# Window attention with channels split 128 and 64, sums copied by sixths for the output projection, and transposes set a piece ahead of the weighted sums

## The chip, the cores and the metric

The kernel runs on one core of a Trainium2 chip. The metric is the time of one execution on the device, in microseconds (us), a median of runs. Everything is fp32.

## The reference, cut to what matters

The network takes an image batch of 8 samples, 56 x 56 pixels, 192 channels, and runs four residual layers. Layers 0 and 1 are Toeplitz mixers, layer 2 is a ConvNeXt block, and layer 3 is a window attention. Each gets its input normalized by groups of six channels (`_gn`). The change concerns layer 3 alone:

```python
x = jnp.roll(x, (-3, -3), (1, 2))                  # x is the group-normalized input
q, k, v = (a.reshape(b, 6, nw, 49, 32) for a in (x @ Wq, x @ Wk, x @ Wv))
scores = jnp.einsum('bhnqd,bhnkd->bhnqk', q, k) * 32 ** 0.5 + bias   # with two masks
attn = jax.nn.softmax(scores, axis=-1)
out = jnp.einsum('bhnqk,bhnkd->bhnqd', attn, v).reshape(b, n_h, n_w, -1)
out = jnp.roll(out @ Wfc + bfc, (3, 3), (1, 2))    # then added to the layer's input
```

The reshape of `q`, `k` and `v` is a plain one: it reads a sample's 3136 tokens of 192 numbers as one row of numbers and cuts it anew into 6 heads of 64 windows of 49 vectors of 32. So one token holds six vectors of 32 ("sixths"), and a window takes 49 vectors that follow one another in that row. The output `out` is read back in the same way, so the output projection again contracts six vectors of 32 for every token.

## The kernel before, in words

Layers 0 to 2 (`tno_layers`, `convnext`) are as they were and come first. `attention` then runs 16 units: the 8 samples, and for each two halves `hh`. A unit is four strips `i` of seven image rows (392 tokens each), one strip from every quarter of the image, so that the four strips fill four groups of 32 partitions. The 192 channels lie as two blocks of 96 (`CH = 96`, `chunked`).

`project(b, hh)` is a generator, so its pieces can be laid between others. It loads the strips to `raw` (`L916`), normalizes and rolls them to `xr` (`L57` on VectorE for the first block of channels, `L928` on ScalarE for the second), and yields. Then it makes the values: for each strip four matmuls over each block of channels (`L938`, 98 tokens stationary, 192 columns), a copy to `vs` on ScalarE (`L946`), a store to DRAM (`vd`, `L948`) and loads of `v` that cut the tokens anew into windows (`L959`). Then, after a yield each, queries and keys (`L973`): for each sixth, half of the strip and block of channels four matmuls, one for each strip, 32 output columns each, side by side in the four column groups. The results go to `f`, laid out token by token with the six sixths inside (`L985` on VectorE, `L983` on ScalarE).

Attention proper runs by thirds `g` of 16 windows in each strip. `scores` multiplies queries and keys (`L997`), adds the bias (`L1009`), and does the softmax: maximum (`L1018`, VectorE), difference (`L1019`, GpSimd), exponential (`L1020`, ScalarE), sum and reciprocal (`L1022`, `L1023`, VectorE), product (`L1024`, GpSimd). `weighted` transposes the result (`L1034`), copies it to `et` (`L1044` on VectorE for one half, `L1042` on ScalarE for the other), multiplies it with the values (`L1052`) and copies the sums to `ot` (`L1059`, VectorE), where, as in `f`, the sixth is the inner index. `out` projects to the 192 channels (`L1071`): for each block of 96 channels and each sixth, four matmuls of 32 rows, one for each strip, side by side in the row groups; the moving operand is

```python
oj = ot.rearrange("p (t j) -> p t j", j=6)
...
oj[qd, :, j],
```

every sixth number of a partition. Then VectorE adds bias and residual in place into `raw` (`L1083`), and `raw` goes to the output (`L1090`).

The order of the pieces is written out by hand in the loop over units. In each third come the scores of the unit; in the first third the previous unit's `out`; then one step of the next unit's `project`; then `weighted` of the third before. What is left of `project` runs before the last `weighted`. Every engine works in program order; a PSUM tile (`bank2`) is two banks, and there are four of them, used in turn. All loads and stores of the attention are issued from one queue (SP), also in order, and a load or store that must wait for something holds up those behind it.

Of the kernel before, what the change touches and what calls it, by code (L numbers as in the profile page):

```python
# [12 lines left out]
F32 = mybir.dt.float32  # L13
AF = mybir.ActivationFunctionType
ALU = mybir.AluOpType
# [7 lines left out]
CH = 96  # L23
# [14 lines left out]
def chunked(ap):  # L38

    return ap.rearrange("(k p) t -> p k t", p=CH)  # L40


class Net:
# [11 lines left out]

    def gn_apply(self, out, x, gn, b, k):
        self.nc.vector.tensor_scalar(  # L57
            out, x, gn[:, k, b, 0:1], gn[:, k, b, 1:2], ALU.mult, ALU.add
        )
# [800 lines left out]
    def attention(self, L, xs, gnd, ys, vd):  # L860
# [6 lines left out]
        ST = HT // 4  # L867
# [3 lines left out]
        with tc.tile_pool(name="at", bufs=2) as p, tc.tile_pool(  # L871
# [4 lines left out]
            gn = one("gn", [CH, 2, B, 2])  # L876
            for b in range(B):
                nc.sync.dma_start(gn[:, :, b, :], chunked(gnd[b * C : (b + 1) * C, :]))
            ws = []
            for n in ("Wq", "Wk", "Wv"):  # L880
                w = one(n, [CH, 2, C])
                nc.sync.dma_start(w, chunked(inp[f"{L}_{n}"]))
                ws.append(w)
# [5 lines left out]
            bfc = one("bfc", [CH, 2])  # L889
# [16 lines left out]

            def project(b, hh):

                raw = p.tile([CH, 2, 4, 7, W], F32, name="raw", bufs=3)
                for i in range(4):
                    r = 14 * i + 7 * hh + 3
                    for a, n in ((0, 7),) if r + 7 <= H else ((0, H - r), (H - r, 7 - H + r)):
                        at = (r + a) % H * W
                        nc.sync.dma_start(  # L916
                            raw[:, :, i, a : a + n, :].rearrange("p k h w -> p k (h w)"),
                            chunked(xs[b])[:, :, at : at + n * W],
                        )
                xr = p.tile([CH, 2, 4 * 7, W], F32, name="xr", bufs=1)  # L920
                rw = raw.rearrange("p k i h w -> p k (i h) w")
                for k in range(2):
                    for c, n, c2 in ((3, 53, 0), (0, 3, 53)):
                        to, of = xr[:, k, :, c2 : c2 + n], rw[:, k, :, c : c + n]
                        if k == 0:
                            self.gn_apply(to, of, gn, b, k)
                        else:
                            nc.scalar.activation(  # L928
                                to, of, AF.Identity, bias=gn[:, k, b, 1:2], scale=gn[:, k, b, 0:1]
                            )  # L930
                xf = xr.rearrange("p k h w -> p k (h w)")
                yield
                v = p.tile([128, 4, 24, 32], F32, name="v", bufs=2)
                for i in range(4):
                    pv = bank2()
                    for s in range(4):
                        for k in range(2):
                            nc.tensor.matmul(  # L938
                                pv[:ST, s // 2, s % 2 * C : (s % 2 + 1) * C],
                                xf[:, k, i * HT + s * ST : i * HT + (s + 1) * ST],  # L940
                                ws[2][:, k, :],
                                start=k == 0,
                                stop=k == 1,
                            )
                    vs = p.tile([ST, 2, 2 * C], F32, name="vs", bufs=3)
                    nc.scalar.copy(vs, pv[:ST, :, : 2 * C])  # L946
                    t0 = i * (T // 4) + hh * HT
                    nc.sync.dma_start(  # L948
                        vd[b][t0 : t0 + HT, :].rearrange("(s p) d -> p s d", p=ST),
                        vs.rearrange("p a (c d) -> p (a c) d", d=C),  # L950
                    )
                    for par in range(2):
                        for q0, n in ((0, 48), (48, 1)):
                            of = bass.AP(
                                vd[b].tensor,
                                vd[b].offset + t0 * C + (WR * par + q0) * 32,
                                [[32, n], [2 * WR * 32, 24], [1, 32]],
                            )
                            nc.sync.dma_start(v[64 * par + q0 : 64 * par + q0 + n, i], of)  # L959
                fs = []  # L960
                for m in range(2):
                    yield
                    f = p.tile([128, HR + 16], F32, name=f"f{m}", bufs=2)
                    if m == 0:
                        nc.gpsimd.memset(f[:, HR:], 0.0)
                    for th in range(2):
                        for j0, nj in ((0, 4), (4, 2)):
                            pq = bank2()
                            for j in range(nj):
                                for k in range(2):  # L970
                                    for i in range(4):
                                        t0 = i * HT + th * (HT // 2)
                                        nc.tensor.matmul(  # L973
                                            pq[32 * i : 32 * i + 32, j // 2, j % 2 * 196 : (j % 2 + 1) * 196],
                                            ws[m][:, k, 32 * (j0 + j) : 32 * (j0 + j) + 32],
                                            xf[:, k, t0 : t0 + HT // 2],
                                            start=k == 0,
                                            stop=k == 1,
                                        )
                            to = view(f, th * (HR // 2) + j0, [[6, 196], [2, nj // 2], [1, 2]])  # L980
                            of = view(pq, 0, [[1, 196], [512, nj // 2], [196, 2]])
                            if j0:
                                nc.scalar.copy(to, of)  # L983
                            else:
                                nc.vector.tensor_copy(to, of)  # L985
                    fs.append(f)
                return raw, v, fs[0], fs[1]

            def scores(hh, g, i, qf, kf):

# [29 lines left out]
                nc.scalar.activation(e3, e3, AF.Exp)  # L1020
                sm = p.tile([128, 16], F32, name="sm", bufs=6)
# [3 lines left out]
                return e  # L1025

            def weighted(g, es, v, ot):

                po = bank2()
                for i in range(2):  # L1030
                    pt = bank2()
                    for c in range(2):
                        for m in range(4):
                            nc.tensor.transpose(  # L1034
                                pt[:113, c, m * 128 : m * 128 + 113],
                                es[i].rearrange("p c n k -> p c (n k)")[:113, c, m * 128 : m * 128 + 113],
                                self.ident[:113, :113],
                            )
                    et = p.tile([113, 8, 113], F32, name="et", bufs=3)
                    ev = pt.rearrange("p c (m q) -> p (c m) q", q=128)[:113, :, :113]  # L1040
                    if i:
                        nc.scalar.copy(et, ev)  # L1042
                    else:
                        nc.vector.tensor_copy(et, ev)  # L1044
# [17 lines left out]
                )  # L1062

            def out(b, hh, raw, ot):
                oj = ot.rearrange("p (t j) -> p t j", j=6)
                for k in range(2):
                    fs = [bank2(), bank2()]
                    for j in range(6):
                        for i in range(4):
                            qd = slice(32 * i, 32 * i + 32)  # L1070
                            nc.tensor.matmul(  # L1071
                                fs[i // 2][:CH, i % 2, :HT],
                                wfc[qd, j, k * CH : (k + 1) * CH],
                                oj[qd, :, j],
                                start=j == 0,
                                stop=j == 5,
                            )
                    for i in range(4):

                        for c, n, c2 in ((0, 53, 3), (53, 3, 0)):  # L1080
                            to = raw[:, k, i, :, c2 : c2 + n]
                            of = fs[i // 2][:CH, i % 2, :HT].rearrange("p (h w) -> p h w", w=W)
                            nc.vector.scalar_tensor_tensor(  # L1083
                                to, of[:, :, c : c + n], bfc[:, k : k + 1], to, ALU.add, ALU.add
                            )
                for i in range(4):
                    r = 14 * i + 7 * hh + 3
                    for a, n in ((0, 7),) if r + 7 <= H else ((0, H - r), (H - r, 7 - H + r)):
                        at = (r + a) % H * W
                        nc.sync.dma_start(  # L1090
# [186 lines left out]
```

## Time and profile before

| what | value |
|---|---|
| time, median of 3 | 6828.79 us (6823.43 to 6830.44) |
| span of the profiled execution | 6818.4 us |
| TensorE busy with matmuls, whole span | 6075.2 us (89%) |
| first scores of the attention start at | 5691.2 us |
| mean granted TensorE clock, whole span | 0.932 |

The busiest groups of the attention, 5600 us to the end, are `L1071` (269.1 us), `L938` (174.9 us), `L973` for the queries (157.2 us) and for the keys (138.8 us). A busy time of TensorE counts a stretch once, however many matmuls run side by side in it, and a matmul's record in the profile is longer than the time after which the next may start; so rates are better taken from how many records pass in a stretch of the chain of waits. One fp32 matmul leaves two records there. In a group's line, "32*96" is rows by columns of the array, "32x392" the operand that streams through.

### The profile page before, as it was taken

What the parts mean: (1) busy time and instruction counts of PE and PEld (TensorE: products, weight loads), DVE (VectorE), ACT (ScalarE), POOL (GpSimd) and SP (SyncE); (2) the same over time, 40 slices, a digit from 0 to 9 for tenths busy, and PEclk for the clock granted to TensorE, in tenths of its full rate; (3) what the DMA queues carried; (4) which work ended last, traced back from release to release, by engine and by line L of the source; (5) the groups of instructions that cost most, each with busy time, mean ns of one, the idle gap of its engine ahead of it and who ended that gap; (6) DMA issues with size and microseconds to landing.
All of it is one profiled execution on the core that took longest, in us unless ns stands there. A gap on an engine that the chain in (4) does not pass through costs nothing.

```text
span 6818.4 us, 150579 instructions
## 1 busy us (share of the span) xinstructions
PE 6075.2 (89%) x68076; PEld 4712.2 (69%) x68076; DVE 2921.2 (43%) x4778; ACT 2033.1 (30%) x2730; POOL 616.1 (9%) x806
## 2 busy tenths in 40 slices
PE   5999878988998898898888899989988997999998
PEld 4777766777777787776777778854475446666665
DVE  6555544443554443555344344250125014444454
ACT  2344432223443222443232222223322332222221
POOL 0000000000000000000000000000000002222222
PEclk9999998988999888999888999999989998999998
DMA  7459886676675676765877654631172114232231
GB/s 240 118 163 249 238 211 186 188 192 176 184 199 166 179 210 193 178 202 161 218 212 213 176 177 139 225 101 41 45 250 95 41 45 94 59 81 66 59 87 38
DMA packets 1223457, 1038.86 MB, mean 152 GB/s; under 512 B 453265, under 2 KB 1180609, under 8 KB 1208737
## 3 DMA queue, kind: packets, MB, share of 16 engines
q1 hardware_dynamic: 810248, 599.79, 31.1%
q10 hardware_dynamic: 378648, 247.74, 13.9%
q0 software_dynamic: 33920, 181.71, 8.5%
q8 instruction: 535, 8.77, 0.5%
q14 instruction: 106, 0.86, 0.0%
HBM read 692.26 MB, written 336.85 MB: 151 GB/s over the span
## 4 chain that ended last, share of the span: by engine, by line
PE 73%; DVE 9%; DMA 6%; ACT 5%; issue 4%; ACTq 2%; SPq 1%; POOL 0%; DVEq 0%; POOLq 0%
PE bank L233 14%; PE pp L789 6%; PE bank L446 5%; PE bank L347 5%; PE bank L456 5%; PE bank L330 5%; PE bank L973 4%; PE pc L708 4%; PE bank L1071 4%; PE po L812 4%; PE bank L461 2%; PE bank L938 2%; PE po L817 2%; PE bank L478 2%; DVE t L242 2%
## 5 line engine op out<-in xcount | busy, mean ns | idle before, releaser
L233 PE MATMUL bank<-wq,t 64*128 64x256 f32 (+5 forms) x8000 | 1318.7, 372 | 63.5 <-ACT ot L337 48.8
L233 PEld LDWEIGHTS bank<-wq,t 64*128 64x128 f32 (+3 forms) x8000 | 1039.7, 189 | 316.6 <-issue 101.8
L242 DVE TENSOR_TENSOR t<-bank,wq 128x1024 f32<-128x1024 f32 (+2 forms) x500 | 540.3, 1113 | 502.6 <-PE bank L233 501.4
L347 PE MATMUL bank<-ident,ot 120*128 120x120 f32 x4032 | 562.2, 303 | 204.1 <-DVE s L350 52.9
L278 ACT ACTIVATE t<-t 128x2048 f32<-128x2048 f32 (+1 forms) x300 | 438.4, 1480 | 972.2 <-DVE t L242 809.5
L347 PEld LDWEIGHTS bank<-ident,ot 120*128 120x128 f32 x4032 | 501.4, 161 | 270.8 <-DVE s L350 65.4
L330 PE MATMUL bank<-q,tm 56*64 56x112 f32 x18432 | 518.5, 265 | 73.8 <-issue 35.3
L330 PEld LDWEIGHTS bank<-q,tm 56*64 56x64 f32 x18432 | 480.0, 138 | 108.7 <-issue 56.0
L490 ACT ACTIVATE t<-bank,wo 128x448 f32<-128x448 f32 x448 | 247.7, 635 | 1020.3 <-PE bank L461 728.2
L497 DVE TENSOR_TENSOR t<-t,t 128x896 f32<-128x896 f32 x224 | 241.1, 1088 | 678.5 <-ACT t L490 676.6
L337 ACT COPY ot<-bank 128x896 f32<-128x896 f32 x576 | 481.7, 917 | 100.6 <-PE bank L330 99.7
L446 PE MATMUL bank<-t,wo 128*128 128x224 f32 x1792 | 414.6, 388 | 77.6 <-ACT t L490 45.8
L789 PE MATMUL pp<-z,w 64*128 64x448 f32 (+1 forms) x1344 | 454.8, 562 | 0.0
L446 PEld LDWEIGHTS bank<-t,wo 128*128 128x128 f32 x1792 | 363.5, 210 | 111.4 <-ACT t L490 46.8
L254 DVE TENSOR_TENSOR t<-t 128x1024 f32<-128x1024 f32 (+1 forms) x300 | 280.7, 954 | 302.5 <-ACT t L278 263.0
L456 PE MATMUL bank<-t,wo 128*128 128x224 f32 x1792 | 367.8, 358 | 6.2 <-DVE t L497 6.0
L456 PEld LDWEIGHTS bank<-t,wo 128*128 128x128 f32 x1792 | 343.8, 193 | 11.0 <-DVE t L497 5.7
L789 PEld LDWEIGHTS pp<-z,w 64*128 64x128 f32 (+1 forms) x1344 | 197.2, 190 | 218.3 <-issue 182.4
L826 DVE TENSOR_TENSOR o<-o,x 128x1344 f32<-128x1344 f32 x28 | 43.6, 1558 | 683.3 <-ACT o L823 683.3
L350 DVE COPY s<-bank 128x784 f32<-128x784 f32 x288 | 264.3, 967 | 132.6 <-PE bank L347 93.0
L353 DVE TENSOR_TENSOR s<-s,bank 128x784 f32<-128x784 f32 x288 | 263.7, 966 | 117.1 <-PE bank L347 117.0
L708 PE MATMUL pc<-xt,cm 112*112 112x108 f32 (+2 forms) x3072 | 307.1, 262 | 0.9 <-issue 0.9
(136 smaller groups left out, 7226.6 us busy)
## 6 DMA issues: line engine op xcount, KB each, us to landing
q<-qv ACTq DMA_DIRECT2D x36, 3584.0 KB
L_sum<-s POOLq DMA_DIRECT2D x288, 392.0 KB, 7.2
t<-L_sum SPq DMA_DIRECT2D x112, 1008.0 KB
qv<-t SPq DMA_DIRECT2D x192, 512.0 KB
cm<-in_L_cm SPq DMA_DIRECT2D x96, 896.0 KB
tm<-L_tab ACTq DMA_DIRECT2D x144, 392.0 KB
q<-qv SPq DMA_DIRECT2D x36, 1568.0 KB
q<-qv ACTq DMA_DIRECT2D x36, 1568.0 KB
```

What stands on the lines that cost most here:

```text
L233: nc.tensor.matmul(pp[:m, b, 256 * j : 256 * j + k], x[rows, j, 2 if part else b, s : s + m], w[rows, part, c0 + c : c0 + c + k],  start=p ...
L242: nc.vector.tensor_add(z[:m, c : c + k, :], view(pp[:m], 0, [[1, k], [256, 4]]), view(bias[:m], c0 + c, [[1, k], [0, 4]]),)
L254: nc.vector.tensor_mul(prod[:m, :k], half[:, :, 0], half[:, :, 1])
L278: nc.scalar.activation(z[:m, :k, :], z[:m, :k, :], AF.Silu)
L330: nc.tensor.matmul(pt[64 * s : 64 * s + 64, r, j * 112 : (j + 1) * 112], tm[rows, c * H : c * H + 64], q[rows, PR * s : PR * s + PR, 4 * c ...
L337: nc.scalar.copy(view(ot, 4 * g, [[112 * 32, 2], [32, 112], [1, 4]]), view(pt, 0, [[512, 2], [1, 112], [112, 4]]),)
L347: nc.tensor.transpose(pz[:, i, :120], ot[:120, at : at + 128], self.ident[:120, :120])
L446: mm(gs[c // 2][:, b, c % 2 * 256 : c % 2 * 256 + N], pw[:, 0, 128 * c : 128 * c + 128], xn[:, b], start=c % 2 == 0, stop=False,)
L456: mm(P[:, b, :N], ow[:, c, 0:128], g[:, 4 * b + c], start=c == 0, stop=False)
L708: nc.tensor.matmul(pc[:, i, 4 * m0 : 4 * m1], cm[:112, i % 4, k, :], xt[:, m0 - 1 + k : m1 - 1 + k, g + i, :], start=n == 0 and i % 4 == 0 ...
L789: nc.tensor.matmul(phs[c, s], w0[rows, part, 128 * c : 128 * c + 128], z[rows, Z[2 if part else s], :], start=part == flip, stop=part != flip,
L812: nc.tensor.matmul(po[s], w1[:, c, 0:128], h[:, s, c, :], start=c == 0, stop=c == 5)
```

## The change

The channels are split 128 and 64 in place of 96 and 96, as the layer before leaves its group norm (`gn3`). The first 128 stand in `xa`, and the last 64 twice in `xb`: partitions 0 to 63 hold rows 0 to 3 of each strip, partitions 64 to 127 rows 3 to 6. A matmul over 128 channels uses the whole height of the array; those over 64 channels use one half of its rows each, so that the two halves of a strip can go side by side. In the output projection, 128 channels are made at once for the whole strip, and the last 64 in two column groups, one for each half of a strip.

`weighted` now also copies the sums from `ot` to `oj` on ScalarE, one sixth after the other, so that the output projection streams numbers that lie side by side. `scores` is cut in two (`divide` holds the second part of the softmax), and `weighted` too: `turned` transposes and copies to `et`, and a piece of the projection stands between it and the matmuls with the values. All three thirds of a unit are now one third late, so the last `weighted` of a unit falls in the first third of the next, and `out` in its second, in two parts. Loading and normalizing are taken out of `project`: the rows for the unit after next are loaded in the second third and normalized at the end of the third third. They come in three large transfers (a few more at the image's edge) in place of four or five. The values' loads are fewer too, and `v` has three buffers.

The weights on the host are laid out to match. The diff, cut to its core:

```diff
+            xa, xb = one("xa", [128, 30 * W]), one("xb", [128, 18 * W])
+            nc.gpsimd.memset(xa[:, 28 * W :], 0.0)
+            nc.gpsimd.memset(xb[:, 16 * W :], 0.0)
+
...
+            def load(b, hh):
+                ra = p.tile([128, 4, 7, W], F32, name="ra", bufs=3)
+                rb = p.tile([128, 4, 4, W], F32, name="rb", bufs=3)
+                rows(b, hh, ra, rb, (xs, nc.sync.dma_start), 0)
+                return ra, rb
+
+            def normalize(b, ra, rb):
+
+                ja, sa = b % 4, b // 4
+                for c, n, c2 in ((3, 53, 0), (0, 3, 53)):
+                    nc.vector.tensor_scalar(
+                        view(xa, c2, [[W, 28], [1, n]]),
+                        view(ra, c, [[W, 28], [1, n]]),
+                        gn3[:, ja, sa, 0:1],
+                        gn3[:, ja, sa, 1:2],
+                        ALU.mult,
+                        ALU.add,
+                    )
+                    nc.scalar.activation(
+                        view(xb, c2, [[W, 16], [1, n]]),
+                        view(rb, c, [[W, 16], [1, n]]),
+                        AF.Identity,
+                        bias=gr[:, b, 1:2],
+                        scale=gr[:, b, 0:1],
+                    )
+
...
                 for i in range(4):
                     pv = bank2()
                     for s in range(4):
-                        for k in range(2):
-                            nc.tensor.matmul(
-                                pv[:ST, s // 2, s % 2 * C : (s % 2 + 1) * C],
-                                xf[:, k, i * HT + s * ST : i * HT + (s + 1) * ST],
-                                ws[2][:, k, :],
-                                start=k == 0,
-                                stop=k == 1,
-                            )
-                    vs = p.tile([ST, 2, 2 * C], F32, name="vs", bufs=3)
-                    nc.scalar.copy(vs, pv[:ST, :, : 2 * C])
-                    t0 = i * (T // 4) + hh * HT
+                        nc.tensor.matmul(
+                            pv[:ST, s // 2, s % 2 * C : (s % 2 + 1) * C],
+                            xa[:, i * HT + s * ST : i * HT + (s + 1) * ST],
+                            ws[2][:, 0, :],
+                            start=s % 2 == 0,
+                            stop=False,
+                        )
+                    for s in (0, 2, 1, 3):
+                        th = s // 2
+                        at = i * LT + th * W + s % 2 * ST
+                        nc.tensor.matmul(
+                            pv[:ST, th, s % 2 * C : (s % 2 + 1) * C],
+                            xb[HALF[th], at : at + ST],
+                            ws[2][HALF[th], 1, :],
+                            start=False,
+                            stop=s % 2 == 1,
+                        )
+                    vs = p.tile([ST, 4, C], F32, name="vs", bufs=3)
+                    nc.scalar.copy(
+                        vs.rearrange("p (a c) d -> p a (c d)", a=2), pv[:ST, :, : 2 * C]
+                    )
+                    t0 = tok(i)
                     nc.sync.dma_start(
-                        vd[b][t0 : t0 + HT, :].rearrange("(s p) d -> p s d", p=ST),
-                        vs.rearrange("p a (c d) -> p (a c) d", d=C),
+                        vd[b][t0 : t0 + 3 * ST, :].rearrange("(s p) d -> p s d", p=ST), vs[:, 0:3]
                     )
+                    nc.sync.dma_start(vd[b][t0 + 3 * ST : t0 + HT, :], vs[:W, 3])
...
+                    for j0 in range(0, 6, 2):
+                        pq = bank2()
+                        for part in range(2):
+                            for j in range(2):
+                                for th, n in ((0, LT), (1, MT)):
                                     for i in range(4):
-                                        t0 = i * HT + th * (HT // 2)
+                                        at = 32 * (j0 + j)
                                         nc.tensor.matmul(
-                                            pq[32 * i : 32 * i + 32, j // 2, j % 2 * 196 : (j % 2 + 1) * 196],
-                                            ws[m][:, k, 32 * (j0 + j) : 32 * (j0 + j) + 32],
-                                            xf[:, k, t0 : t0 + HT // 2],
-                                            start=k == 0,
-                                            stop=k == 1,
+                                            pq[32 * i : 32 * i + 32, th, j * LT : j * LT + n],
+                                            ws[m][HALF[th] if part else slice(0, 128), part, at : at + 32],
+                                            xb[HALF[th], i * LT + th * W : i * LT + th * W + n]
+                                            if part
+                                            else xa[:, i * HT + th * LT : i * HT + th * LT + n],
+                                            start=part == 0 and j == 0,
+                                            stop=part == 1 and j == 1,
                                         )
-                            to = view(f, th * (HR // 2) + j0, [[6, 196], [2, nj // 2], [1, 2]])
-                            of = view(pq, 0, [[1, 196], [512, nj // 2], [196, 2]])
-                            if j0:
+                        for th, n in ((0, LT), (1, MT)):
+                            to = view(f, th * LT * 6 + j0, [[6, n], [1, 2]])
+                            of = view(pq, th * 512, [[1, n], [LT, 2]])
+                            if th:
                                 nc.scalar.copy(to, of)
                             else:
                                 nc.vector.tensor_copy(to, of)
+                        if (m, j0) in ((0, 0), (0, 4)):
+                            yield
                     fs.append(f)
-                return raw, v, fs[0], fs[1]
+                return v, fs[0], fs[1]
 
...
@@ -1018,30 +1073,38 @@
                 nc.vector.tensor_reduce(mx, e3, AX.X, ALU.max)
                 nc.gpsimd.tensor_sub(e3, e3, view(mx, 0, [[1, 16], [0, WR]]))
                 nc.scalar.activation(e3, e3, AF.Exp)
+                return e
+
+            def divide(e):
+
+                e3 = e.rearrange("p c n k -> p (c n) k")[:, :, :WR]
                 sm = p.tile([128, 16], F32, name="sm", bufs=6)
                 nc.vector.tensor_reduce(sm, e3, AX.X, ALU.add)
                 nc.vector.reciprocal(sm, sm)
                 nc.gpsimd.tensor_mul(e3, e3, view(sm, 0, [[1, 16], [0, WR]]))
...
+            def turned(e, i):
+                pt = bank2()
+                for c in range(2):
...
+                return et
+
+            def weighted(g, ets, v, ot, oj):
+                    et = ets[i]
...
-
-            def out(b, hh, raw, ot):
-                oj = ot.rearrange("p (t j) -> p t j", j=6)
-                for k in range(2):
+                t0, t1 = 16 * WR * g // 6, 16 * WR * (g + 1) // 6
+                nc.scalar.copy(
+                    view(oj, t0, [[HT, 6], [1, t1 - t0]]), view(ot, 6 * t0, [[1, 6], [6, t1 - t0]])
+                )
+
+            def out(b, hh, ra, rb, oj):
+                for k, raw, n in ((0, ra, 7), (1, rb, 4)):
                     fs = [bank2(), bank2()]
                     for j in range(6):
                         for i in range(4):
                             qd = slice(32 * i, 32 * i + 32)
-                            nc.tensor.matmul(
-                                fs[i // 2][:CH, i % 2, :HT],
-                                wfc[qd, j, k * CH : (k + 1) * CH],
-                                oj[qd, :, j],
-                                start=j == 0,
-                                stop=j == 5,
+                            for h in range(k + 1):
+                                nc.tensor.matmul(
+                                    fs[i // 2][HALF[h] if k else slice(0, 128), i % 2, : n * W],
+                                    wfc[qd, j, 128 * k : 128 * k + 128 - 64 * k],
+                                    oj[qd, j, h * MT : h * MT + n * W],
+                                    start=j == 0,
+                                    stop=j == 5,
+                                )
...
+                        for c, m, c2 in ((0, 53, 3), (53, 3, 0)):
+                            to = raw[:, i, :, c2 : c2 + m]
+                            nc.vector.scalar_tensor_tensor(
+                                to,
+                                view(fs[i // 2], i % 2 * 512 + c, [[W, n], [1, m]]),
+                                bfc[:, k : k + 1],
+                                to,
+                                ALU.add,
+                                ALU.add,
                             )
...
+                    if k == 0:
+                        yield
+                rows(b, hh, ra, rb, (ys, lambda t, d: nc.sync.dma_start(d, t)), 1)
...
+            raws = {0: load(*units[0])}
+            normalize(units[0][0], *raws[0])
             gen = project(*units[0])
             now = None
             while now is None:
                 now = step(gen)
-            late = None
-            for n, (b, hh) in enumerate(units):
-                raw, v, qf, kf = now
+            raws[1] = load(*units[1])
+            normalize(units[1][0], *raws[1])
+            late = outs = None
+            for n in range(len(units) + 1):
+                if n < len(units):
+                    (b, hh), (v, qf, kf) = units[n], now
                 gen = project(*units[n + 1]) if n + 1 < len(units) else None
                 now = None
-                ot = p.tile([128, HR], F32, name="ot")
-                pending = None
                 for g in range(NG):
-                    es = [scores(hh, g, i, qf, kf) for i in range(2)]
+                    es = [scores(hh, g, i, qf, kf) for i in range(2)] if n < len(units) else []
+                    if g == 1 and n:
+                        outs = out(*units[n - 1], *raws.pop(n - 1), oj)
+                        step(outs)
+                    elif gen is not None and now is None:
+                        now = step(gen)
+                    for e in es:
+                        divide(e)
                     if late is not None:
-                        out(*late)
-                        late = None
+                        g_late, es_late, v_late = late
+                        ets = [turned(e, i) for i, e in enumerate(es_late)]
+                    if g == 1 and n:
+                        step(outs)
                     if gen is not None and now is None:
                         now = step(gen)
-                    if pending is not None:
-                        weighted(*pending)
-                    pending = (g, es, v, ot)
-                while gen is not None and now is None:
-                    now = step(gen)
-                weighted(*pending)
-                late = (b, hh, raw, ot)
-            out(*late)
+                    if late is not None:
+                        if g_late == 0:
+                            ot = p.tile([128, HR], F32, name="ot", bufs=1)
+                            oj = p.tile([128, 6, HT], F32, name="oj", bufs=1)
+                        weighted(g_late, ets, v_late, ot, oj)
+                    late = (g, es, v) if es else None
+                    if g == 1 and n + 2 < len(units):
+                        raws[n + 2] = load(*units[n + 2])
+                    if g == 2 and n + 2 < len(units):
+                        normalize(units[n + 2][0], *raws[n + 2])
```

## The prediction

> **What bounds the kernel now.** I read the page first, for where the attention lies: GpSimd works only in the last sixth of the span, where the softmax runs.
>
> ```profile
> PE 6075.2 (89%) x68076; PEld 4712.2 (69%) x68076; DVE 2921.2 (43%) x4778; ACT 2033.1 (30%) x2730; POOL 616.1 (9%) x806
> ...
> POOL 0000000000000000000000000000000002222222
> ```
>
> The change touches nothing else, so all else keeps its time. Next, busy time by window over fourteen whole units (one sample, one half of the rows), from the first output projection at 5747.5 us to the fifteenth, then four short windows (columns: length, busy PE, PEld, DVE, ACT, POOL, granted clock, DMA share, GB/s).
>
> ```profile
> 5747.50:6742.40 994.90, 914.90 (x19044) 647.68 (x19048) 496.25 (x727) 206.82 (x264) 256.21 (x181) 0.93 0.29 69
> ```
> ```profile
> 5815.20:5831.90 16.70, 16.70 (x103) 4.74 (x104) 9.99 (x18) 1.75 (x2) 6.03 (x4) 1.00 0.00 1
> 6173.30:6190.00 16.70, 16.70 (x99) 5.43 (x97) 8.27 (x16) 1.75 (x2) 6.04 (x4) 0.83 0.01 2
> 5785.80:5793.90 8.10, 8.10 (x195) 6.12 (x193) 7.02 (x10) 2.19 (x3) 5.74 (x5) 1.00 0.64 116
> 6212.20:6222.50 10.30, 10.30 (x197) 6.76 (x193) 7.00 (x9) 2.28 (x3) 6.19 (x5) 0.78 0.50 92
> ```
>
> A unit takes 994.9/14 = 71.06 us, and TensorE is busy for 92% of it; VectorE has 50%. TensorE bounds. The second pair of lines is the projection to Wq, the first pair the output projection. The Wq piece grows from 8.1 to 10.3 us when the clock falls to 0.78; the output projection takes 16.7 us at 1.00 and at 0.83 alike. So it isn't bound by the array. Third, the chain of waits in one stretch, for the clean length of each piece:
>
> ```profile
> 5785.83 8.11 PE bank L973 x192
> ...
> 5794.96 1.11 DVE et L1044
> ...
> 5800.36 7.43 PE bank L973 x174
> ...
> 5808.81 1.11 DVE et L1044
> ...
> 5811.97 0.92 ACT et L1042
> ...
> 5815.26 16.62 PE bank L1071 x96
> ```
>
> The trace has two records for each fp32 matmul. L973 puts four matmuls of 32 columns side by side: 192 records are 48 slots in 8.11 us, 169 ns for 196 columns, 0.86 ns a column. L1071 puts four matmuls of 32 rows side by side: 96 records are 24 slots in 16.62 us, 692 ns for 392 columns, 1.77 ns a column, twice as much. What differs is the operand: L973 reads `xf` contiguously, L1071 reads `ot` with a step of six floats. Between pieces TensorE waits for `et`, 3.1 us in this stretch.
>
> Last, the timeline of weight loads in an earlier stage, where 64-row matmuls are already used as the change will use them:
>
> ```profile
> 5401.48 0.19 PEld L789 LDWEIGHTS pp<-z,w 128*128 128x128 f32 x1 [0.19 <-issue]
> 5401.85 0.19 PEld L789 LDWEIGHTS pp<-z,w 128*128 128x128 f32 x1 [0.18 <-issue]
> 5402.69 0.30 PEld L789 LDWEIGHTS pp<-z,w 64*128 64x128 f32 x4 [0.65 <-issue]
> 5403.18 0.19 PEld L789 LDWEIGHTS pp<-z,w 64*128 64x128 f32 x2 [0.18 <-issue]
> 5403.55 0.19 PEld L789 LDWEIGHTS pp<-z,w 64*128 64x128 f32 x2 [0.18 <-issue]
> ```
>
> Full-height matmuls start every 0.37 us, 64-row ones two every 0.37 us: the row halves work together. Where the shape changes, 0.1 us more passes (0.49 instead of 0.37 to the next pair).
>
> [...]
>
> **The change part by part, on TensorE, for one unit.**
>
> Output projection. Now 24 slots of 692 ns, 16.6 us. The sums are copied to `oj`, one sixth after another, so the reads are contiguous. Channels 0 to 127: 6 sixths x 2 records = 12 slots of 392 columns at 0.85 ns, 4.0 us. Channels 128 to 191 as two row halves of 64, eight 32x64 tiles at once: 12 slots of 224 columns, 196 ns each, 2.35 us. Together 6.3 us: 10.3 saved. Bounds: if the step isn't the cause, 12 x 692 + 12 x 396 = 13.0 us; if the eight tiles run as four, 8.7 us. I take 6.3, because of the clock test above.
>
> Values. Now 64 records of 165 ns (96 contracted channels twice, x64 in 10.59 us on the chain), 10.6 us. After: per quarter 8 records over 128 channels and 4 paired slots over 64, 12 x 165 ns, and two changes of shape at 0.1: 2.2 us; four quarters 8.7 us. 1.9 saved; nothing if the pairs don't overlap.
>
> Queries and keys. Now 96 slots of 169 to 171 ns, 16.4 us. After: six groups. In each, the 128 channels cost two sixths x two records x (224 columns, 190 ns, and 168 columns, 146 ns) = 1.34 us; the 64 channels run both row halves at once, 4 x 190 ns = 0.76 us; two changes of shape 0.2. 2.3 x 6 = 13.8 us. 2.6 saved; minus 0.9 if the halves run one after the other.
>
> Scores, transposes and weighted sums keep their matmuls. The sum saved is 10.3 + 1.9 + 2.6 = 14.8 us of a unit, 236 us for 16.
>
> Waits. `turned` now stands a piece of projection ahead of `weighted`, so the copy of `et` (1.10 us on VectorE, 0.91 on ScalarE) lies beside that piece. Those waits, some 3 to 4 us a unit, should go. But a new one comes in the second third. VectorE has, in order: two biases and maxima (4 x 0.97), eight additions of the first projection part (4 x 0.59 + 4 x 0.23 = 3.3), two sums with reciprocals (2.4), then `et`. Counting from the start of that third, TensorE ends the transposes at about 8.4 us, while VectorE gets to `et` at 12.3. Behind it queue the second projection part (its second PSUM pair comes free with the additions, about 9.8), the next projection piece (its PSUM buffer is the one that `et` frees, 13.4), and the weighted sums. That is 3.3 us of standing, then about 1 us where VectorE's normalization sits ahead of the next scores and 1 us for ScalarE's copies of `vs` behind the exponentials. Old waits out, 5.3 us and small change in: I put the net at 0.
>
> Other engines. VectorE keeps about 37 us a unit (the additions shrink by 0.8, the copies of `f` stay); ScalarE goes from 14.8 to some 18 with three copies of 128x784 to `oj` (0.9 us each by its other copies, 1.6 if the step of six costs it as it costs TensorE); both fit within 56 us. The copy to `oj` of the last third lies behind the next scores (1.9 us of TensorE); half a microsecond may show, inside the 5.
>
> Transfers. Raw rows for unit n+2 now use the buffers of unit n-1, so the load waits on the SP queue for that unit's store. The additions end about 16 us into the second third; store and load at up to 5 us each and their issue at 0.3 to 0.5 us bring the rows by about 30, and the normalization comes at 36. Hidden by 6 us. What queues behind them on SP is only the next unit's `vd` stores, later still.
>
> Ends. Three issues in place of 12 before the first normalization (now 8.6 us of queue): 4 us saved. The final output projection is one of the 16.
>
> Sum: 6828.8 - 236 - 4 = 6589, say 6590 us; a unit at 56.3 us.
>
> **The rivals.**
> *The waits take back a third of it.* VectorE at 37 us in order inside 56 leaves little room, and if each third shows what I found in one, a unit takes 61 us: 6590 + 16 x 4.7 = 6665 us. For it: in-order VectorE between projection and softmax. Against: the first and last third have no additions. Chance 0.18.
> *The step isn't the cause.* Four row groups might be slow by themselves; then the output projection takes 13.0 us, and 6590 + 16 x 6.7 = 6697 us. For it: no contiguous 32-row matmul with 392 columns is in the trace. Against: the clock test. Chance 0.07.
> *The waits fall as well.* On the chain a third's scores take 1.9 us, eight transposes 0.98, half a weighted sum 0.83: 5.7, 5.9 and 5.0 us a unit. All pieces are then 60.2 us now and 45.4 after. Now 71.06 - 60.2 = 10.9 us are waits, halved clock and the ends of pieces; the forecast leaves as much. If the clock stays up with denser work, only my 5.5 us of waits are left and a unit takes 51 us: 6590 - 16 x 5.3 = 6505 us. Chance 0.09.
> *Slower.* The step isn't the cause, and neither the 64-row halves nor eight tiles overlap: output 8.3 + 9.4, values 11.4, queries and keys 17.3, 46.4 us against 43.6 now; if 1 us more is waited, 3.8 x 16 = 61: 6890 us. For it: eight tiles are untested. Against: the L789 pairs. Chance 0.04.
>
> **How the numbers follow.** The forecast has 0.62, with its own spread of some 40 us either way for the net of the waits and the clock. Below 6530 lies most of the third rival, above 6670 most of the second and the slower one; what is left out is about 0.2. Faster 0.95 (all but the last case and a remainder), same 0.01, slower 0.04.
>
> **What would show it.** Output projection: two pieces of about 4.0 and 2.4 us, no longer 16.6. Queries and keys about 13.8, values 8.7 us a unit. Unit period 56 us. Waits of TensorE for `et` gone from the first and last thirds, and a wait of about 3 us in the second, released by VectorE. No wait of VectorE for the raw rows. Wrong if the output matmuls stay at 1.77 ns a column, if 64-row matmuls start one by one, or if TensorE's idle share grows beyond 20%.

## The result, and the profile after

The changed kernel takes 6675.88 us (median of 4 runs, 6663.55 to 6683.01) beside 6829.61 us (before, with one run more than in the table ahead): a ratio of 0.9772, 95% interval 0.9753 to 0.9791. It is 154 us faster; 239 were forecast. Of the span's busy times, TensorE's alone fell by much, from 6075.2 to 5903.1 us:

```profile
PE 5903.1 (88%) x68844; PEld 4630.6 (69%) x68844; DVE 2902.7 (44%) x4810; ACT 2112.7 (32%) x2810; POOL 616.1 (9%) x808
```

Busy time of fourteen whole units, from the first to the fifteenth output projection (the same columns as before: length, PE, PEld, DVE, ACT, POOL, clock, DMA, GB/s):

```profile
5761.40:6618.60 857.20, 746.31 (x19649) 565.89 (x19648) 478.71 (x754) 273.98 (x330) 254.65 (x180) 0.87 0.38 79
```

A unit takes 857.2/14 = 61.23 us; 56.3 were forecast, 71.06 it was. TensorE is busy for 87% of it, no longer 92%, and its mean clock is 0.87, no longer 0.93. So the work fell as planned, and something came in its place. What TensorE waited for in this stretch (us in all, times, longest):

```profile
PE bank L1052 <- issue: 75.7, 39, 5.8
...
PE bank L1138 <- DVE ra L1149: 14.8, 21, 1.5
PE bank L1115 <- issue: 11.9, 11, 2.7
...
PE bank L1115 <- DVE et L1100: 0.5, 1, 0.5
```

L1052 is now the scores, L1138 the output projection, L1115 the weighted sums. In the fourteen units before, the scores were L997 and the weighted sums L1052, and these were their waits:

```profile
PE bank L1052 <- DVE et L1044: 35.9, 28, 1.3
...
PE bank L1052 <- issue: 18.2, 17, 1.2
PE bank L997 <- issue: 13.9, 11, 2.3
PE bank L1052 <- ACT et L1042: 6.2, 21, 0.3
```

The waits for `et` are gone (0.5 us in all). The wait on VectorE in the second third is there, at 14.8/14 = 1.1 us. But the scores now stand 75.7 us in 39 waits that nothing in the profile releases. The chain of waits at the turn of one unit shows where they are:

```profile
6044.06 1.46 PE bank L1115 x116
6045.52 1.14 issue
6046.66 0.28 PE bank L1115 x5
6046.94 1.83 PE bank L1052 x111
6048.77 1.46 issue
6050.23 0.46 PE bank L1052 x4
6050.69 2.83 PE bank L967 x8
6053.52 1.56 PE bank L977 x8
```

TensorE stops inside the weighted sums and inside the scores, between instructions that wait for no other engine. And the values that follow (L967, L977) take 2.83 and 1.56 us, though the same pieces take 1.30 to 1.49 and 0.84 at full clock. Three windows: one with both stops; one that begins inside an earlier stop, at half clock throughout; and the one that follows it, at full clock, which holds the first of the two stops and ends inside the second:

```profile
6043.00:6055.00 12.00, 9.40 (x316) 7.65 (x304) 7.87 (x10) 4.38 (x6) 3.56 (x3) 0.76 0.02 4
6025.30:6032.20 6.90, 4.70 (x92) 3.18 (x100) 3.08 (x4) 1.16 (x2) 2.34 (x3) 0.51 0.42 109
6032.20:6049.20 17.00, 15.43 (x554) 11.25 (x539) 9.52 (x15) 6.62 (x10) 3.85 (x3) 1.00 0.01 4
```

What TensorE waits for lies in the list of DMA queues (a packet is one piece of a transfer). Its line for TensorE's instructions, after (before it had 535 packets):

```profile
q8 instruction: 541, 8.86, 0.6%
```

The change adds 68844 - 68076 = 768 matmul records and as many weight loads, 1536 instructions, and 6 packets: 256 instructions a packet. (A later run with 6144 instructions fewer has 24 packets fewer, the same.) Its packets in the raw trace around the two stops, start and end in us:

```
6034.08 6035.00
6039.51 6040.46
6044.35 6045.31
6047.94 6048.90
6051.39 6052.54
```

Each stop ends 1.3 to 1.4 us after a packet has landed (6045.31 to 6046.66, 6048.90 to 6050.23). In none of the eleven traces of this case do two packets start less than 3.21 us apart. The weighted sums and the scores of a third are 256 instructions each, 1.5 to 1.7 and 1.9 us without a stop, and the change puts them back to back: 512 instructions in some 3.5 us, where at one packet in 3.2 us two packets' worth takes 6.4. Before, transposes and a wait for `et` stood in the middle of this stretch, and 384 instructions came behind them.

### The profile page after: what moved, and what is told of

The parts are those of the page before. It is cut to its first block, busy times and chain, and to the rows that moved or that the text cites. A ratio compares the mean times of both kernels' runs of the same rounds, so it can differ in the third digit from the quotient of the medians.

```text
span 6671.3 us, 152109 instructions
## 1 busy us (share of the span) xinstructions
PE 5903.1 (88%) x68844; PEld 4630.6 (69%) x68844; DVE 2902.7 (44%) x4810; ACT 2112.7 (32%) x2810; POOL 616.1 (9%) x808
## 4 chain that ended last, share of the span: by engine, by line
PE 71%; DVE 10%; DMA 7%; issue 4%; ACT 4%; ACTq 2%; SPq 1%; POOL 0%; DVEq 0%; POOLq 0%
PE bank L222 15%; PE pp L778 7%; PE bank L336 6%; PE bank L435 5%; PE bank L445 5%; PE bank L319 5%; PE pc L697 4%; PE po L801 4%; PE bank L1022 4%; PE bank L450 2%; PE po L806 2%; PE bank L467 2%; DMA t<-in_x 2%; DVE t L231 1%; PE bank L1052 1%
## 5 line engine op out<-in xcount | busy, mean ns | idle before, releaser
L352 POOL DMA_DIRECT2D L_sum<-s x288 | 141.4, 498 | 1834.8 <-DVE s L342 1793.2
```

## The experiments

Theory A: TensorE outruns its instructions there, and with the standstills comes more half clock. (A standstill, or stop, is idle time of TensorE without a semaphore; half clock is a granted clock of 0.5, the only value beside 1 in these traces. That the one brings the other was my supposition; the windows counted further down bear on it.) Rivals: B, PSUM tiles that VectorE frees late; C, the small packets of the value loads delay the instruction packets. In the table, "stops" are idle times of TensorE of over 0.3 us ahead of an instruction without a semaphore, ending 1.15 to 1.75 us after a packet of instructions, counted in the raw trace; "half" is the time at half clock. All per unit, over fourteen units. Each ratio is to runs of the kernel before taken along with it. The band of 1.15 to 1.75 us isn't what makes the stops: in the kernel after, 53 of the 54 such idle times without a semaphore end in it, and of the 22 idle times with one, none does.

| run | time, us | ratio to before, interval | unit, us | stops, us | half, us |
|---|---|---|---|---|---|
| before | 6829.6 | | 71.06 | 1.4 | 9.5 |
| after | 6675.9 | 0.9772 (0.9753 to 0.9791) | 61.23 | 6.4 | 16.4 |
| e1_spread | 6563.3 | 0.9616 (0.9595 to 0.9638) | 53.85 | 2.7 | 6.1 |
| e2_no_vload | 6670.4 | 0.9766 (0.9745 to 0.9787) | 61.40 | 6.6 | 16.5 |
| e6_filler | 6689.7 | 0.9802 (0.9787 to 0.9816) | 62.35 | 1.3 | 4.9 |
| e9_half_scores | 6590.6 | 0.9671 (0.9643 to 0.9698) | 55.87 | 2.8 | 11.2 |
| e3_sixths_only | 6732.6 | 0.9865 (0.9847 to 0.9882) | 65.38 | 1.5 | 10.0 |
| e4_stride | 6712.7 | 0.9832 (0.9809 to 0.9856) | 63.62 | 5.6 | 13.4 |
| e5_no_ahead | 6676.8 | 0.9782 (0.9762 to 0.9803) | 61.34 | 6.3 | 16.7 |
| e7_values_last | 6542.3 | 0.9576 (0.9546 to 0.9606) | 54.10 | 4.0 | 6.7 |
| e8_interleaved | 6535.8 | 0.9570 (0.9534 to 0.9606) | 52.04 | 2.1 | 3.6 |

**A piece between weighted sums and scores.** In the loop over thirds:

```diff
 es = [scores(hh, g, i, qf, kf) for i in range(2)]
+ets = [turned(e, i) for i, e in enumerate(es_late)]
 now = step(gen)
 ...
-ets = [turned(e, i) for i, e in enumerate(es_late)]
-now = step(gen)
 weighted(g_late, ets, v_late, ot, oj)
+now = step(gen)
```

> Same work as the changed kernel, other order in each third: scores, transposes, first piece, weighted sums, second piece, so that a piece of projection stands between the weighted sums and the next scores. Theory A (TensorE's instructions arrive in blocks of 256, no closer than some 3.4 us; weighted sums and scores, 512 instructions in 3.4 us, outrun them[...]): waits without a semaphore ahead of the scores fall from 5.2 to under 2 us a unit, half clock from 16 to about 10 us, a unit from 61.2 to about 55 us, 6580 us in all. Theory B (the standstills are PSUM tiles that VectorE frees late): VectorE's order hardly changes, 6660 to 6690 us.

The same matmuls in 113 us less. In the chain of waits the values now stand between weighted sums and scores, at full clock, and in this stretch nothing stops:

```profile
6010.33 1.50 PE bank L1115 x125
6011.83 1.49 PE bank L967 x8
6013.31 0.84 PE bank L977 x8
...
6016.47 1.90 PE bank L1052 x116
...
6020.14 7.25 PE bank L1138 x144
```

Of stops 3.7 us a unit go, and of half clock 10.3 us; 8.7 of these lay on busy matmuls, worth half of it, 4.3 us, if work takes twice as long there. That is the 7.4 us a unit that were gained, within 0.6. VectorE's work is the same; this speaks against B.

**Value loads left out.**

```diff
-nc.sync.dma_start(v[64 * par : 64 * par + 48, i], of)
+if (b, hh) == (0, 0):
+    nc.sync.dma_start(v[64 * par : 64 * par + 48, i], of)
```

> The changed kernel, but the values are loaded back from DRAM for the first unit only and used for all (the outputs of the other units use the wrong values); TensorE has the same instructions. Theory C (instruction blocks come late because the small packets of the value loads fill the DMA engines): waits without a semaphore ahead of the scores fall under 2 us a unit, about 6590 us. Theory A (the pace of the blocks itself is too slow for the dense stretch): the waits that are over 3 us shorten, those of 1 to 2 us stay, so 3 to 4.5 us a unit and 6640 to 6665 us.

Nothing moves, though the DMA share falls from 0.38 to 0.21:

```profile
5763.40:6623.00 859.60, 748.35 (x19651) 568.81 (x19649) 479.22 (x754) 275.13 (x330) 255.04 (x181) 0.87 0.21 60
```

The stops stay (6.6 us beside 6.4). C falls, and with it my own guess that the long stops would shorten.

**More work for TensorE.**

```diff
 weighted(g_late, ets, v_late, ot, oj)
+fill = bank2()
+for i in range(4):
+    nc.tensor.matmul(fill[:, i // 2, :448], wfc[:, i, :128], bias.rearrange("p v n k -> p (v n k)")[:, :448], ...)
```

> The changed kernel with four matmuls of 128 rows, 128 and 448 columns more behind the weighted sums of every third; their result is not used. They are 16 instructions and 3.0 us of TensorE, 9 us a unit. If TensorE's time adds up (theory B): 6676 + 47 x 3.0 = 6817 us. Theory A: the instruction blocks arrive while they run, the 5.2 us of standstill and 3 to 4 us of halved clock go, and the time stays within 30 us of 6676 us.

The filler (L1208) takes 3.2 us a third, some 150 us in all, and the kernel is 14 us slower:

```profile
6054.08 3.21 PE bank L1208 x8
6057.29 1.90 PE bank L1052 x125
6059.19 1.48 PE bank L967 x8
```

The scores run through in 1.90 us, the values behind them at full clock. Of the 6.4 us of stops 5 go and of 16.4 us at half clock 11.5. Work put into the stops fills them, so TensorE's time doesn't add up as B had it. Alone this doesn't rule B out: a wait for VectorE that ends at a set time could be filled as well. Against that stand the missing semaphores and the next run.

**Fewer instructions in the same time.**

```diff
 for half in range(2):
-    for c in range(2):
+    for c in range(1):
```

> The changed kernel, its order kept, with the scores of one of the two row groups only, used for both (half of the score matmuls are left out, so the output is not the reference's): 128 in place of 256 instructions in each third. In TensorE's time this is at most 0.95 us a third, 46 us in all: 6630 to 6676 us if TensorE's time adds up (theory B). Theory A: the standstills ahead of the scores (5.2 us a unit) fall under 2 us and the half clock under 10 us a unit, so 100 us or more on top of that: 6530 to 6580 us.

85 us less. In the groups from 5690 us on after, and in the whole of e9, the scores' matmuls:

```profile
L1052 PE MATMUL bank<-f,f 32*64 32x49 f32 x6039 | 123.4, 242 | 83.7 <-issue 83.7
```
```profile
L1052 PE MATMUL bank<-f,f 32*64 32x49 f32 x3072 | 106.5, 232 | 24.8 <-issue 23.7 <-DVE f L1037 1.1
```

Half of the matmuls keep TensorE busy for nearly as long. At full clock and without a stop a third's scores take 1.88 us in e9, two tiles at a time, and 1.97 in e6 and e1, four at a time (first start to last end). So hardly 5 of the 85 us are work; with the rest go 3.6 us a unit of stops and 5.2 us at half clock. PSUM tiles and VectorE's work are those of the kernel after, so with B the stops would have stayed: B falls as the main cause. A's figures were met for the stops ahead of the scores alone (1.7 us), not for the half clock (11.2 us, under 10 expected), and the time lies 11 us above what A gave; waits on VectorE and for `oj` grew to 2.1 us a unit.

**The copy by sixths alone**, in the kernel before:

```diff
+nc.scalar.copy(view(oj, t0, [[HT, 6], [1, t1 - t0]]), view(ot, 6 * t0, [[1, 6], [6, t1 - t0]]))
 ...
-oj[qd, :, j],
+oj[qd, j, :],
```

> The kernel before with one part of the change: the sums are copied by sixths and the output projection reads the copies; 96 and 96 channels and the old order stay. If the step of six is the cause of the slow output projection: 24 slots of 334 in place of 692 ns, 8.0 us in place of 16.6, 8.6 x 16 = 138 us less, 6692 us; under theory A up to 20 us of it are given back, because the halved clock now costs something in the output projection too. If the step is not the cause: 6829 us or more.

94 us of the 138. In the chain of waits the output projection of a unit, 96 records as before, now takes 8.15 us in place of 16.62 at full clock:

```profile
5742.40 8.15 PE bank L1074 x96
```

So the step is the cause, and the 44 us that are missing are two new costs: the wait for `oj`, 12.9/14 = 0.9 us a unit, and half clock in the output projection. Before, that piece took 16.7 us at either clock; now it takes 8.15 us at full clock and up to 11.0 where part of it runs at half, and 2.5 us a unit lie at half clock, worth 1.3. The stops don't grow (1.5 us beside 1.4).

**The copy undone**, in the kernel after:

```diff
-oj[qd, j, h * MT : h * MT + n * W],
+oj.rearrange("p (t j) -> p t j", j=6)[qd, h * MT : h * MT + n * W, j],
 ...
-oj = p.tile([128, 6, HT], F32, name="oj", bufs=1)
+oj = ot
```

> The changed kernel with the copy by sixths undone: the output projection reads the sums with a step of six, in the new split of channels. If the step alone is the cause of the slow output projection: 12 slots of 692 and 12 of about 396 ns in place of 334 and 196 ns, 6.7 us a unit, 6676 + 107 = 6783 us. If the gain of the output projection came from the split of channels instead: 6676 us or less, since three copies on ScalarE go.

The output projection's busy time grows, in the groups of the two kernels (the whole span, e4 first):

```profile
L1134 PE MATMUL bank<-ot,wfc 32*128 32x392 f32 x768 | 139.8, 871 | 2.1 <-DVE ot L1122 1.1 <-issue 1.0
L1134 PE MATMUL bank<-ot,wfc 32*64 32x224 f32 x1536 | 93.5, 569 | 2.8 <-DVE ra L1145 2.7
```
```profile
L1138 PE MATMUL bank<-oj,wfc 32*128 32x392 f32 x768 | 97.5, 660 | 6.3 <-ACT oj L1127 5.1 <-issue 1.3
L1138 PE MATMUL bank<-oj,wfc 32*64 32x224 f32 x1536 | 57.7, 400 | 15.8 <-DVE ra L1149 15.4 <-issue 0.3
```

That is 233.3 beside 155.2 us, 78 more (107 were expected), of which 37 reach the time: the waits ahead of L1138 (22 us) shrink to 5, and half clock falls by 3 us a unit. Both ways of asking give the copy less than its matmuls save: 94 us in the old order, 37 in the new one.

**Transposes back beside the weighted sums**: `turned` moved to just ahead of `weighted`, behind the second piece.

> The changed kernel with the transposes right ahead of the weighted sums, behind the second piece. The prediction's reckoning: the copies of et stand on the path again, 3 to 4 us a unit, 6725 to 6740 us. Theory A: the transposes are sparse in instructions (32 in 2 us), and so is the wait for et, so the blocks get ahead before the weighted sums and scores; of the 6.4 us of standstill without a semaphore 2 to 3 us go, and the clock is down no longer than now: 6670 to 6710 us.

No difference (6676.8 beside 6675.9 us). Waits for `et` come back, 19.0 us in fourteen units, 1.4 a unit and not the 3 to 4 that I reckoned, probably since the transposes of both halves now stand together; the VectorE waits of the output projection go:

```profile
PE bank L1052 <- issue: 86.5, 42, 3.6
PE bank L1115 <- DVE et L1100: 19.0, 41, 0.5
```

Here I had A wrong too: the transposes' sparse 1.8 us ahead of 512 dense instructions, it seems, give too little time, and the stops stay at 6.3 us.

**Two steps on from e1_spread.** First the queries and keys ahead of the values in `project`, which is also cut into pieces at other places; then scores and transposes in halves by turns (`for i in range(2): scores(...); turned(...)`).

> The order of e1_spread, and in the projection the queries and keys ahead of the values, so that the piece ahead of the next unit's scores is one that they don't wait for. Theory A: in e1_spread the scores still wait about 1 us a unit for the keys' copies[...]; without it 1 to 2 us a unit less, 6535 to 6550 us. If the clock falls from something other than standstills, e1_spread's 6563 us stays.

> e7_values_last with the two halves of the scores and the two transposes taken in turn (scores, transposes, scores, transposes), so that the densest stretch of instructions is 128 in 0.95 us. Theory A: the waits without a semaphore of e7_values_last, 4.0 us a unit, fall to 2 to 3, 6515 to 6535 us. If what is left there is not the pace of the blocks: 6540 us as before, or more, since the maximum of the second half starts 1 us later.

6542.3 and 6535.8 us. The intervals of their ratios overlap with each other and, slightly, with that of e1_spread (6563.3 us), so only the gain over the kernel after is clear. In e7 the wait for the keys' copies (14.5 us in e1) is gone, but stops grew from 2.7 to 4.0 us, perhaps as dense pieces moved next to each other. In e8 they are down to 2.1. Both kernels beat the changed one, e8 by 140 us, with the same matmuls. From 6100 to 6500 us of e8 TensorE is busy 95% at a clock of 0.98:

```profile
6100.00:6500.00 400.00, 378.29 (x10948) 291.74 (x10933) 260.23 (x423) 153.74 (x184) 144.54 (x102) 0.98 0.44 98
```

## Why the prediction was wrong, point by point

*What bounds the kernel* was right: TensorE, and the step of six in the output projection.

*The sum on TensorE* held nearly. At full clock a strip of values takes 2.3 us (2.2 said), a group of queries or keys 2.3 (2.3). The two parts of the output projection together take 6.73 us on the chain of e8 (6.3 said): four tiles at once take 329 ns (333 said) and eight 189 ns (196 said), the usual step in all fourteen units of e1 and e8; the rest is the first slots of a part and its end. The 64-row halves do run two at once.

*The step that failed is the waits: "I put the net at 0".* The figures ahead of it don't even give 0: 3 to 4 us go out and 5.3 come in. The old waits did go (3.0 us a unit for `et`, now none), and the new one on VectorE came at 1.1 us in place of 3.3. But the working followed only semaphores and PSUM. Taking the transposes out of the middle left 512 dense instructions in a row, and TensorE stops there: 6.4 us of stops a unit, 1.4 before. Its own instructions are the resource that ran out. e1 shows it with the same matmuls in another order, e6 by work added at little cost, e9 by instructions removed that took almost no time; e2 shows that the load on the DMA engines isn't why. No run puts the transposes back between the halves; ahead of both halves (e5) they don't help. All idle time of TensorE together rose from 71.06 - 914.90/14 = 5.7 us a unit to 61.23 - 746.31/14 = 7.9.

*The clock was the second half of it: "the forecast leaves as much".* The prediction left 10.9 us a unit for waits, halved clock and the ends of pieces. The kernel before spent 9.5 us a unit at half clock, 8.9 of them on busy matmuls, of which 2.1 in the output projection, which didn't feel it; after it was 16.4 us, 14.6 of them on busy matmuls. If work there takes twice as long, as the Wq piece of the prediction shows (10.3 us at 0.78 are worth 8.0 at full clock, and 8.1 were measured there), half clock cost 6.8/2 = 3.4 us before and 14.6/2 = 7.3 after. So of the 4.9 us a unit that the forecast missed, 2.2 are more idle time and 3.9 more half clock, less some 1.2 in what is left. The prediction even used the output projection's insensitivity as its evidence, and didn't draw that the gain there would expose the clock.

Do the stops lower the clock? In these units stretches of one clock last whole multiples of 3.41 us (33 whole stretches before, of 1 to 28 times that, and 77 after, of 1 to 12). I cut the full-clock time of the fourteen units of all eleven traces into such windows and took the share of each in which TensorE was idle:

| idle share of a full-clock window | windows | followed by half clock |
|---|---|---|
| under 20% | 1753 | 5 |
| 20 to 30% | 133 | 28 |
| 30 to 40% | 173 | 80 |
| 40 to 50% | 94 | 77 |
| 50% or more | 94 | 93 |

So idle windows go ahead of half clock, the more often the more idle they are. The counts show no sharp threshold: windows idle for 30 to 50% were followed by half clock in 157 of 267 cases, and from 30% on it was 38 of 44 in the kernel after, but only 12 of 38 in the kernel before and 13 of 45 in e3_sixths_only, which has the old order. No run holds the stops and frees the clock, so that the stops cause the drop is likely and not shown, and the shares above are worked out and not separated by a run.

*The rivals.* The second one, waits taking back a third, names almost the measured time (6665 us, 61 us a unit), but by chance: it puts the time into waits on VectorE, and those were 1.1 us. The third one, a clock that stays up, says 51 us a unit; e8, with most of the stops gone, comes to 52.0. *VectorE, ScalarE and the transfers* were right: none is near its bound, no wait on the raw rows shows. A copy to `oj` takes 1.6 us, the upper of the two values.

What stays open is what sets the 3.2 to 3.4 us between the closest packets of instructions, when each takes about 1.0 us, what lowers the clock, and why the first four units of e8 take 55 us at a clock of 0.93 and the others 51 at 0.98.

## What to carry to other kernels

Count instructions as a load of their own: where many small matmuls follow each other, compare their number per microsecond with the pace at which the trace shows instruction packets arriving (here 256 instructions in 3.21 us at the closest), and put long matmuls between dense stretches (in e1_spread the stops fell from 6.4 to 2.7 us a unit). Idle time of TensorE put down to nothing, ending a nearly fixed time after an instruction packet (here 1.15 to 1.75 us), is the sign. When waits or sparse pieces are taken out of a dense stretch, ask what they gave time to: here, it seems, to the next instructions. And when a piece gets fast that was slow for another reason than the clock, ask what it covered: here a low clock, which then cost time (the output projection of e3_sixths_only took 8.15 us at full clock and up to 11.0 with part of it at half).

## What the runs showed of the hardware

The traces have one instruction packet for every 256 instructions of TensorE (6 more packets with 1536 instructions more, 24 fewer with 6144 fewer), and in none of the eleven do two start less than 3.21 us apart, which comes to at most 80 instructions a microsecond. The stops were nearly the same at a DMA share of 0.38 and of 0.21 (6.4 and 6.6 us a unit). Where TensorE stood for over 0.3 us without a semaphore, it started again 1.15 to 1.75 us after a packet had landed, in 393 of 404 cases. A window of 3.41 us in which it was idle for half the time or more was followed by half clock in 93 of 94 cases. Eight tiles of 32 rows and 64 columns run at once: sets of eight records with 224 fp32 columns start every 189 ns, and sets of four tiles of 32 rows and 128 columns with 392 every 329 ns. A ScalarE copy of 128 x 786 numbers that reads with a step of six takes 1.60 us, where an exponential of 128 x 784 read without such a step takes 0.87. Halving the number of score tiles at work at once left their time nearly as it was (1.88 us for half of a third's matmuls, 1.97 for all).
